# Output products of batches 0 to 6 as seven half-size products, and another order of the last batch's blocks, stores and products

## The chip, the cores and the metric

The kernel runs on one core of one Trainium2 chip. The metric is the device time of one launch in microseconds (us); lower is better. Engines: TensorE (PE, matrix products; its weight loads are listed as PEld), VectorE (DVE), ScalarE (ACT), GpSimd (POOL) and SyncE (SP, which here only issues transfers). Matrix products write to PSUM banks of 128 x 512 f32 numbers.

## The reference

Attention with shared queries, keys and values over 8 batches of 1024 tokens with 512 features and 8 heads, where a 0/1 mask says which tokens count; the result is added to the input. All is f32.

```python
xt = jnp.transpose(x, (0, 2, 1))                     # x: (8, 512, 1024)
q = xt @ Wq.T
qh = q.reshape(B, T, NH, dk).transpose(0, 2, 1, 3)   # NH = 8, dk = 64
scores = scale * jnp.einsum('bhqd,bhkd->bhqk', qh, qh)
logits = (scores * cmask + (1.0 - cmask) * NEG) * rmask
attn = jax.nn.softmax(logits, axis=-1)
ctx = jnp.einsum('bhqk,bhkd->bhqd', attn, qh)
out = ctx.transpose(0, 2, 1, 3).reshape(B, T, D) @ Wo.T
return x + jnp.transpose(out, (0, 2, 1))
```

A masked-out row gets the same mean value for all its keys, so the kernel works on the kept tokens of a batch (about half) and one token that stands for all others.

## The kernel before, in words

**Tokens.** Each batch has room for 544 tokens (SHORT): four blocks of 128 and a strip of 32 (block LAST), with 544/2 = 272 queries in each half. If a batch keeps more, a second program with 576 (LONG) runs instead; it is built from the same functions.

**Pairs.** Two heads (128 features) of one batch are a pair (b, pr): 32 pairs, pr from 0 to 3. One loop runs over them, and its order of instructions is written by hand; each engine works through its own queue in that order. A pair has five slots k = 0 to 4. In each slot PE makes the scores of one block of keys (L684, strip first: L706) and ACT their exponentials (L692). Between them `slots_of` lists other work by slot, of neighbouring pairs and batches: the projection of the pair after next (`project`, L598), its transposed values (L626), lengths and a bias from them (L645 to L667), the weighted values of the pair before (`begin_attend`, `go_on_attend`, `end_attend`, L730 and L748), the gathered tokens of the next batch (`collect`).

**Sums and contexts.** `invert` inverts a pair's sums of exponentials on DVE, sends the row through DRAM and reads it back on all partitions (row and rb, SP's queue). Two pairs later `contexts` (L859 to L868) multiplies the weighted values by it; the result cT holds 128 features x 544 tokens. For the pair before the last, `spread` does this with PE and ACT instead (L810, L817).

**Outputs.** `output(b, i)` multiplies block i of the four cT tiles with woT (the transposed Wo, 512 features; L883), ACT copies the PSUM bank to a tile oc (L892), and POOL's queue stores it to DRAM as od (L894). For a block of 128 tokens that is four matmuls with 512 columns each, for the strip 16 small ones with 128 columns, four side by side. Outputs of batch b - 1 run in slot 3 of pairs (b, 1): blocks 0, 1 and LAST; (b, 2): block 2; (b, 3): block 3. In the last batch, b = 7, they run in (7, 1) and (7, 2). PSUM banks come in two rings of two, tags t and a; weighted values use a, nearly all else t.

**Back to the input.** `load_rows` reads rows of x (transposed) into g, `fetch` (L977, POOL) gathers od by token and adds it to g in the transfer, `finish_blocks` (L947, DVE) transposes g back, and SP stores a batch (L954, list `rests`). Tables say which of the eight blocks goes where, by (pr, k): FETCH and FINISH for batch b - 2, and FETCH_LAST, FINISH_LAST, ROWS_LAST for batch 6 in the last batch. Ahead of each fetch `keep_step` (L974) makes POOL wait for that slot's exponentials.

**The end.** Batch 7 has no later pairs. In pair (7, 3) `begin_output` multiplies blocks with the first three cT tiles (L903) and ACT keeps the partial sums; after `attend_last`, `end_output` adds the last product (L919, DVE L927) and SP stores od (L933). Then eight gathers (L963), PE transposes (L992), additions to x (L993) and stores (L994).

## Time and profile before

| | |
|---|---|
| time, median of 3 runs | 656.38 us (655.18 to 656.91) |
| profiled execution, its own time | 656.09 us |
| its span in the profile | 654.4 us |
| busy: PE, DVE, ACT, POOL | 614.3, 359.8, 378.3, 211.1 us |
| DMA | 116.62 MB, mean 178 GB/s |

The profile is of one execution. The span is from the first to the last instruction recorded; 1.7 us of the execution's time lie outside it. Busy times are the union of an engine's instructions. In the timeline a row is a start, a duration, the engine, the line of the kernel, the operation with the tiles written and read, the count of instructions merged into the row, and in brackets how long the engine had been idle and what ended that. In the groups by line the columns are busy time, mean ns of one, and idle time before them with its causes.

### The profile page before, as it was taken

The numbers are of one execution on the slowest core, as the hardware profiler recorded it, in microseconds if no ns is written. First come the engines' busy times: TensorE is split into PE (matmuls) and PEld (weight loads), VectorE is DVE, ScalarE is ACT, GpSimd is POOL, SyncE is SP. The second block draws the span as 40 slices with busy tenths as digits, with TensorE's granted clock in tenths as the row PEclk, the third lists the DMA queues.
The fourth block names the chain that finished last, engine by engine and source line by source line (L and its number), as shares of the span: only waits on it lengthen the run. The fifth ranks groups of instructions, "written<-read, shape, count | busy, mean of one in ns | idle before, by whom it ended". The sixth has DMA issues, their size and how long they took to land. (4 is left out here: it accounts for less than half of the span.)

```text
span 654.4 us, 15913 instructions
## 1 busy us (share of the span) xinstructions
PE 614.3 (94%) x6078; PEld 380.5 (58%) x6078; DVE 359.8 (55%) x1034; ACT 378.3 (58%) x1004; POOL 211.1 (32%) x313
## 2 busy tenths in 40 slices
PE   4789799999999999999999999999999999998964
PEld 3756466656665666566665666566665666554323
DVE  6449556335465566746465558566575425444543
ACT  4266558754766577754776577664775556554400
POOL 5620400140067004830176004720275006305422
PEclk7799899999999999999999999999999999999985
DMA  7666612454588757977598756975795635566677
GB/s 237 187 199 166 233 57 67 141 168 133 147 178 214 244 172 186 180 246 230 172 182 257 228 173 155 199 244 187 196 179 164 198 102 94 111 162 188 112 220 219
DMA packets 94543, 116.62 MB, mean 178 GB/s; under 512 B 11911, under 2 KB 61639, under 8 KB 94462
## 3 DMA queue, kind: packets, MB, share of 16 engines
q1 hardware_dynamic: 74030, 75.20, 38.6%
q0 software_dynamic: 16208, 38.25, 25.2%
q10 hardware_dynamic: 4224, 2.10, 1.1%
q8 instruction: 49, 0.80, 0.5%
q14 instruction: 32, 0.26, 0.1%
HBM read 72.81 MB, written 42.70 MB: 177 GB/s over the span
## 5 line engine op out<-in xcount | busy, mean ns | idle before, releaser
L692 ACT ACTIVATE e<-s,bias 128x544 f32<-128x544 f32 x256 | 180.5, 710 | 75.6 <-PE s L684 58.9
L684 PE MATMUL s<-qT 64*64 64x272 f32 x2048 | 154.8, 398 | 6.5 <-ACT e L692 4.9
L748 PE MATMUL av<-e,v 64*64 64x272 f32 x1920 | 132.4, 392 | 0.0
L598 PE MATMUL pq<-xc,wqT 128*128 128x272 f32 x512 | 131.4, 401 | 0.0
L598 PEld LDWEIGHTS pq<-xc,wqT 128*128 128x128 f32 x512 | 93.3, 190 | 36.8 <-issue 21.0
L684 PEld LDWEIGHTS s<-qT 64*64 64x64 f32 x2048 | 77.2, 133 | 55.8 <-ACT e L692 13.4
L883 PE MATMUL po<-woT,cT 128*128 128x512 f32 (+1 forms) x448 | 108.9, 439 | 0.0
L894 POOL DMA_DIRECT2D od<-oc x56 | 30.2, 544 | 238.5 <-ACT oc L892 237.7
L977 POOL DMA_INDIRECT g<-od,block_origin x56 | 90.1, 1610 | 30.9 <-DVE ends L721 8.1
L748 PEld LDWEIGHTS av<-e,v 64*64 64x64 f32 x1920 | 76.6, 134 | 38.1 <-issue 2.1
L664 DVE TENSOR_REDUCE m<-pq 128x1 f32<-128x128 f32 x28 | 8.2, 292 | 132.0 <-ACT qT L610 107.5
L883 PEld LDWEIGHTS po<-woT,cT 128*128 128x128 f32 (+1 forms) x448 | 46.5, 149 | 54.6 <-issue 53.2
L608 ACT COPY qT<-pq 128x272 f32<-128x272 f32 x64 | 24.6, 385 | 69.7 <-PE pq L655 29.0
L947 DVE STREAM_TRANSPOSE xr<-g 128x512 f32<-128x512 f32 x56 | 57.9, 1099 | 7.6 <-DMA g<-od,block_origin 7.5
L645 DVE TENSOR_REDUCE len<-sq 128x10 f32<-128x640 f32 x32 | 25.8, 805 | 60.4 <-ACT sq L643 60.3
L974 POOL COPY step<-e 1x1 f32<-1x1 f32 x75 | 23.7, 316 | 90.7 <-ACT e L692 90.5
L692 ACT ACTIVATION_READ_ACCUMULATOR e<-s,bias 128x1 f32 x256 | 50.5, 197 | 0.0
L544 POOL DMA_INDIRECT xin<-xd,source x40 | 38.7, 968 | 16.6 <-issue 5.6
L892 ACT COPY oc<-po 128x512 f32<-128x512 f32 (+1 forms) x35 | 18.0, 515 | 44.0 <-PE po L883 43.5
L474 DVE STREAM_TRANSPOSE xt<-x 128x1024 f32<-128x1024 f32 x28 | 34.7, 1241 | 1.5 <-DMA xd<-xt 0.9
L532 DVE TENSOR_SCALAR_CACHE_REDUCE junk<-rank,key 128x1024 f32<-128x1024 f32 (+4 forms) x35 | 34.9, 998 | 0.0
L721 DVE CUSTOM_DVE_ANT_0 junk<-el,part 128x272 f32<-128x272 f32 x64 | 27.3, 427 | 6.6 <-ACT el L709 4.4
(175 smaller groups left out, 674.0 us busy)
## 6 DMA issues: line engine op xcount, KB each, us to landing
xd<-xt SPq DMA_DIRECT2D x120, 128.0 KB
x<-in_x_dram SPq DMA_DIRECT2D x56, 256.0 KB
g<-xd SPq DMA_DIRECT2D x56, 256.0 KB
out_dram<-xr SPq DMA_DIRECT2D x28, 512.0 KB
rb<-row SPq DMA_DIRECT2D x60, 160.0 KB
od<-oc POOLq DMA_DIRECT2D x28, 256.0 KB
rank<-ranks SPq DMA_DIRECT2D x6, 512.0 KB
x<-in_x_dram POOLq DMA_DIRECT2D x8, 256.0 KB
```

The source lines that it names most:

```text
L474: nc.vector.transpose(xt.rearrange("p k (d f) -> p k d f", d=ND), xs[b][r][:, :, at : at + n].rearrange("p d (k t) -> p k d t", t=Q),)
L532: nc.vector.tensor_scalar(junk[:, :n], rank[:, i * P :], key[:, col], 0.0, ALU.is_le, ALU.add, accum_out=found[:, col])
L544: nc.gpsimd.indirect_dma_start(out=xin[:n, :], out_offset=None, in_=xds[b], in_offset=bass.IndirectOffsetOnAxis(ap=searches[b][2][:n, i : ...
L598: nc.tensor.matmul(pq[:, :KH], wqT[:, d, pr * P : (pr + 1) * P], xcs[b][:, d, cols], start=(d == 0), stop=(d == ND - 1),)
L684: nc.tensor.matmul(ss[h][r * DK : (r + 1) * DK, hf, :KH], qT[heads[h], c * P + r * DK : c * P + (r + 1) * DK], qT[heads[h], queries[hf]], ...
L692: nc.scalar.activation(e[:, :, h, :], ss[h][:, :, :KH], AF.Exp, bias=bias, scale=SCALE, accum_out=sums[pair[1] % 2][:, h, c : c + 1],)
L721: nc.vector.tensor_tensor_reduce(junk[:, :KH], e[:, 0, h, :], parts[b], 1.0, 0.0, ALU.mult, ALU.add, ends[pr % 2][:, h : h + 1])
L748: nc.tensor.matmul(avs[pair][hf][head, :KH], v[keys, c, head], e[keys, hf, h, :], start=(c == 0 and not crossed), stop=(c == LAST - 1 and ...
L883: nc.tensor.matmul(po[k * n : (k + 1) * n, :w], cTs[b, pr][:, i * P : i * P + n], woT[:, pr, k * w : (k + 1) * w], start=(pr == 0), stop=( ...
L894: nc.gpsimd.dma_start(ods[b][places[i], k * w : (k + 1) * w], oc[k * n : (k + 1) * n, :w])
L947: nc.vector.transpose(xr.rearrange("p (d a) (t i) -> p a d t i", a=A, i=NT)[..., i], gs[b, i].rearrange("p (a d f) -> p a d f", a=A, f=Q),)
L977: nc.gpsimd.indirect_dma_start(out=gs[b, i], out_offset=None, in_=ods[b], in_offset=bass.IndirectOffsetOnAxis(ap=block_origin[:, b, i : i ...
```

## The change

The four whole blocks of a batch are a product of 512 tokens x 512 features by 512 x 512 weights. It is split into halves in all three directions, and seven products of half the size, with sums of inputs and outputs around them, take the place of eight (Winograd's form of Strassen's method). It is done for batches 0 to 6 in the SHORT program; the strip of 32 tokens keeps `output`, and batch 7 keeps its four blocks.

- `combine_weights`, once, in pair (1, 0): four differences of quarters of woT on POOL.
- `combine_tokens`: sums s1 to s4 of quarters of cT on DVE, two instructions each, in the tiles of tag xt; in (b, 1), slots 1, 1, 2 and 4.
- `product(b, i)`: eight passes in four matmuls with 256 columns, into one PSUM bank. ACT copies product 1; DVE adds each of the others (product 5 twice); four stores of 256 tokens x 256 features on POOL's queue. Products 1, 6, 7, 5 run in (b, 1), 2 and 3 in (b, 2), 4 in (b, 3). Product 1 is issued ahead of `add_features` (list `leads`). In (b, 1) the second half of the projection uses tag a.
- In the last batch all seven products of batch 6 run in (7, 1), and the strip too; the tables FETCH_SOON, FINISH_SOON, FETCH_LAST, FINISH_LAST and ROWS_LAST put transfers and transposes earlier; `spread` and `contexts` of pair (7, 2) go to slot 0 of (7, 3); the partial products go to slots 1, 2, 3, 4, 4 (before 1, 1, 2, 3, 4), and the strip's are made four side by side (`add_product`), with two of its four stores on ACT's queue.
- In all batches, blocks 4 and 5 of FINISH go from slot 2 to slot 3 of (b, 1).

```diff
         for k in range(parts):
             nc.gpsimd.dma_start(ods[b][places[i], k * w : (k + 1) * w], oc[k * n : (k + 1) * n, :w])
 
+    HALF = D // 2
+    both = {}
+    if n == SHORT:
+        for i in range(1, 5):
+            both["t", i] = keep.tile([P, 2, HALF], F32, name=f"t_{i}")
+
+    def combine_weights():
+
+        left = [woT[:, 0:2, 0:HALF], woT[:, 2:4, 0:HALF]]
+        right = [woT[:, 0:2, HALF:D], woT[:, 2:4, HALF:D]]
+        t1, t2, t3, t4 = (both["t", i] for i in range(1, 5))
+        nc.gpsimd.tensor_tensor(t1, right[0], left[0], ALU.subtract)
+        nc.gpsimd.tensor_tensor(t2, right[1], t1, ALU.subtract)
+        nc.gpsimd.tensor_tensor(t3, right[1], right[0], ALU.subtract)
+        nc.gpsimd.tensor_tensor(t4, t2, left[1], ALU.subtract)
+
+    def combine_tokens(b, i):
+
+        if i in (1, 3):
+            t = sb.tile([P, T // NQ // Q, P], F32, tag="xt", name=f"st_{b}_{i}", bufs=2)
+            t = t.rearrange("p k c -> p (k c)").rearrange("p (s j n) -> p s j n", s=2, j=2)
+            both["s", i], both["s", i + 1] = t[:, 0], t[:, 1]
+        for j in range(2):
+            early, late_ = cTs[b, j], cTs[b, 2 + j]
+            to = both["s", i][:, j, :]
+            upper, lower = slice(0, 2 * P), slice(2 * P, 4 * P)
+            if i == 1:
+                nc.vector.tensor_tensor(to, early[:, lower], late_[:, lower], ALU.add)
+            elif i == 2:
+                nc.vector.tensor_tensor(to, both["s", 1][:, j, :], early[:, upper], ALU.subtract)
+            elif i == 3:
+                nc.vector.tensor_tensor(to, early[:, upper], early[:, lower], ALU.subtract)
+            else:
+                nc.vector.tensor_tensor(to, late_[:, upper], both["s", 2][:, j, :], ALU.subtract)
+
+    def product(b, i):
+
+        def tokens(j, m):
+            cols = slice(m * P, (m + 1) * P)
+            if i in (3, 5, 6, 7):
+                return both["s", {3: 4, 5: 1, 6: 2, 7: 3}[i]][:, j, cols]
+            first = 2 * P if i == 4 else 0
+            cols = slice(first + m * P, first + (m + 1) * P)
+            return cTs[b, j if i == 1 else 2 + j][:, cols]
+
+        def features(j):
+            if i == 1:
+                return woT[:, j, 0:HALF]
+            if i == 2:
+                return woT[:, 2 + j, 0:HALF]
+            if i == 3:
+                return woT[:, 2 + j, HALF:D]
+            return both["t", {4: 4, 5: 1, 6: 2, 7: 3}[i]][:, j, :]
+
+        po = bank(f"po_{b}_{i}")
+        for m in range(2):
+            for j in range(2):
+                nc.tensor.matmul(
+                    po[:, m * HALF : (m + 1) * HALF],
+                    tokens(j, m),
+                    features(j),
+                    start=(j == 0),
+                    stop=(j == 1),
+                )
+
+        def new(name):
+            t = both[name] = sb.tile([P, D], F32, tag="oc", name=f"{name}_{b}", bufs=NC)
+            return t
+
+        def store(t, row, col):
+            rows = slice(END + row * 2 * P, END + (row + 1) * 2 * P)
+            nc.gpsimd.dma_start(
+                ods[b][rows, col * HALF : (col + 1) * HALF].rearrange("(m p) c -> p m c", p=P),
+                t.rearrange("p (m c) -> p m c", m=2),
+            )
+
+        add = nc.vector.tensor_tensor
+        if i == 1:
+            ods[b] = dr.tile([NK, D], F32, tag="od", name=f"od_{b}")
+            nc.scalar.copy(new("c11"), po)
+        elif i == 6:
+            add(new("c12"), po, both["c11"], ALU.add)
+        elif i == 7:
+            add(new("c21"), po, both["c12"], ALU.add)
+        elif i == 5:
+            add(new("c22"), po, both["c21"], ALU.add)
+            add(both["c12"], po, both["c12"], ALU.add)
+            store(both["c22"], 1, 1)
+        elif i == 2:
+            add(both["c11"], po, both["c11"], ALU.add)
+            store(both["c11"], 0, 0)
+        elif i == 3:
+            add(both["c12"], po, both["c12"], ALU.add)
+            store(both["c12"], 0, 1)
+        else:
+            add(both["c21"], both["c21"], po, ALU.subtract)
+            store(both["c21"], 1, 0)
+
     partials = {}
 
+    def add_product(b, i, pr, po, start, stop):
+
+        n = sizes[i]
+        parts = P // n
+        w = D // parts
+        tokens = cTs[b, pr][:, i * P : i * P + n]
+        if parts == 1:
+            nc.tensor.matmul(po, tokens, woT[:, pr, :], start=start, stop=stop)
+            return
+        in_order = woT[:, pr, :].rearrange("p (a d f) -> p d a f", a=A, d=ND)
+        for k in range(parts):
+            nc.tensor.matmul(
+                po[k * n : (k + 1) * n, :w],
+                tokens,
+                in_order[:, k * ND // parts : (k + 1) * ND // parts, :, :],
+                start=start,
+                stop=stop,
+            )
+
     def begin_output(b, i):
 
-        n = sizes[i]
         po = bank(f"pa_{b}_{i}")
         for pr in range(ND - 1):
-            nc.tensor.matmul(
-                po[:n, :],
-                cTs[b, pr][:, i * P : i * P + n],
-                woT[:, pr, :],
-                start=(pr == 0),
-                stop=(pr == ND - 2),
-            )
+            add_product(b, i, pr, po, pr == 0, pr == ND - 2)
+        w = D // (P // sizes[i])
         pa = sb.tile([P, D], F32, tag="xin", name=f"pa_{b}_{i}", bufs=NC)
-        nc.scalar.copy(pa[:n, :], po[:n, :])
+        nc.scalar.copy(pa[:, :w], po[:, :w])
         partials[i] = pa
 
     def end_output(b, i):
         n = sizes[i]
+        parts = P // n
+        w = D // parts
         if i == 0:
             ods[b] = dr.tile([NK, D], F32, tag="od", name=f"od_{b}")
         po = bank(f"po_{b}_{i}")
-        nc.tensor.matmul(
-            po[:n, :],
-            cTs[b, ND - 1][:, i * P : i * P + n],
-            woT[:, ND - 1, :],
-            start=True,
-            stop=True,
-        )
+        add_product(b, i, ND - 1, po, True, True)
         oc = sb.tile([P, D], F32, tag="oc", name=f"oc_{b}_{i}", bufs=NC)
-        nc.vector.tensor_tensor(
-            oc[:n, :].rearrange("p (d a f) -> p a d f", d=ND, a=A),
-            po[:n, :].rearrange("p (a d f) -> p a d f", d=ND, a=A),
-            partials[i][:n, :].rearrange("p (a d f) -> p a d f", d=ND, a=A),
-            ALU.add,
-        )
-        nc.sync.dma_start(ods[b][places[i], :], oc[:n, :])
+        if parts == 1:
+            nc.vector.tensor_tensor(
+                oc.rearrange("p (d a f) -> p a d f", d=ND, a=A),
+                po.rearrange("p (a d f) -> p a d f", d=ND, a=A),
+                partials[i].rearrange("p (a d f) -> p a d f", d=ND, a=A),
+                ALU.add,
+            )
+        else:
+            nc.vector.tensor_tensor(oc[:, :w], po[:, :w], partials[i][:, :w], ALU.add)
+        for k in range(parts):
+            queue = nc.scalar if k % 2 else nc.sync
+            queue.dma_start(ods[b][places[i], k * w : (k + 1) * w], oc[k * n : (k + 1) * n, :w])
 
     def in_blocks(t):
         return t.rearrange("(k f) (a n) -> a f k n", f=Q, a=A)
...
         if before:
             do(0, go_on_attend, before)
         due = []
-        if pr == 1 and b + 1 == B:
-            due = [0, 1]
-        elif pr > 0 and 0 < b < B - 1:
+        if pr == 1 and b + 1 == B and in_halves:
+            for k, i in ((1, 1), (1, 2), (2, 3), (3, 4)):
+                do(k, combine_tokens, b - 1, i)
+        elif pr == 1 and b + 1 == B:
+            due = [1, 2]
+            do(2, output, b - 1, 0)
+        elif pr > 0 and 0 < b < B - 1 and not in_halves:
             due = {1: (0, 1, LAST), 2: (2,), 3: (3,)}[pr]
+        halves = ()
+        if in_halves and 0 < b < B - 1:
+            halves = ((), (1, 6, 7, 5), (2, 3), (4,))[pr]
+            if pr == 1:
+                for k, i in ((1, 1), (1, 2), (2, 3), (4, 4)):
+                    do(k, combine_tokens, b - 1, i)
         if not new:
+            if halves and pr == 1:
+                leads[p] = [lambda: product(b - 1, 1)]
+                halves = halves[1:]
+            for i in halves:
+                do(3, product, b - 1, i)
+            if halves and pr == 1:
+                do(3, output, b - 1, LAST)
             for i in due:
                 do(3, output, b - 1, i)
+        if in_halves and p == ND:
+            do(0, combine_weights)
         if p == 0:
             do(0, project, behind, 1)
             do(1, values, behind)
...
             do(3, collect, b + 1, 3, None, "a")
             do(3, collect, b + 1, 4, by_vector)
             do(3, lengths_of, behind)
+            for i in halves:
+                do(3, product, b - 1, i)
             for i in due:
                 do(3, output, b - 1, i)
             do(3, project_with_top, 0)
...
             do(1, project_with_values)
             do(2, lengths_of, behind)
             do(2, end_attend, before)
-            do(3, project_with_top, 1)
+            if pr == 1 and b + 1 == B and in_halves:
+                for k, i in ((2, 1), (2, 6), (3, 7), (3, 5), (4, 2), (4, 3), (4, 4)):
+                    do(k, product, b - 1, i)
+            do(3, project_with_top, 1, "a" if halves and pr == 1 else "t")
         elif behind:
-            do(1, output, b - 1, LAST - 1)
             do(1, values, behind)
             do(2, lengths_of, behind)
             do(2, end_attend, before)
             do(3, bias_of, behind)
-            do(3, output, b - 1, LAST)
         if p == ND - 1:
             for d in range(ND):
                 do(3 + d // 2, turn_weights, woT, "wo", d, None, "at"[d // 2], True)
         if pr == 1 and b + 1 == B:
-            do(4, output, b - 1, 2)
+            if not in_halves:
+                do(4, output, b - 1, LAST - 1)
+            do(4, output, b - 1, LAST)
         if p + 1 == len(pairs):
             for i in range(NC):
-                do((1, 1, 2, 3, 4)[i], begin_output, b, i)
+                do((1, 2, 3, 4, 4)[i], begin_output, b, i)
         return todo
 
     def load_weights(w, nm, queue=None):
...
             (1, 0): (5,),
             (1, 1): (6, 7),
         }
-        FINISH = {(0, 4): (0, 1), (1, 1): (2, 3), (1, 2): (4, 5), (1, 4): (6, 7)}
-        FETCH_LAST = {(2, 4): (0, 1, 2), (3, 0): (3, 4, 5), (3, 1): (6, 7)}
-        FINISH_LAST = {(3, 1): (0, 1, 2), (3, 2): (3, 4, 5), (3, 3): (6, 7)}
+        FINISH = {(0, 4): (0, 1), (1, 1): (2, 3), (1, 3): (4, 5), (1, 4): (6, 7)}
+        FETCH_SOON = {(0, 0): (0,), (0, 1): (1,), (0, 2): (2,), (0, 3): (3, 4), (0, 4): (5, 6), (1, 0): (7,)}
+        FINISH_SOON = {(0, 2): (0,), (0, 3): (1,), (0, 4): (2,), (1, 0): (3, 4), (1, 1): (5, 6), (1, 2): (7,)}
+        FETCH_LAST = {(2, 0): (0,), (2, 1): (1, 2), (2, 2): (3, 4), (2, 3): (5, 6), (2, 4): (7,)}
+        FINISH_LAST = {(3, 1): (0, 1, 2, 3), (3, 2): (4, 5, 6, 7)}
         ROWS = {(2, 2): (0, 1), (2, 3): (2, 3), (3, 0): (4, 5), (3, 2): (6, 7)}
-        ROWS_LAST = {(2, 0): (0, 1, 2), (2, 1): (3, 4, 5), (2, 2): (6, 7)}
+        ROWS_LAST = {(1, 0): (0, 1, 2), (1, 1): (3, 4), (1, 2): (5, 6), (1, 3): (7,)}
         for p, pair in enumerate(pairs):
             b, pr = pair
             before = pairs[p - 1] if p else None
...
                         invert(before)
                     else:
                         inv = inverses(before)
-                if p + 1 == len(pairs):
-                    if k == 1:
-                        spread(before, inv)
-                        contexts(before)
+                if p + 1 == len(pairs) and k == 0:
+                    spread(before, inv)
+                    contexts(before)
                 if b > 1:
-                    for i in FETCH.get((pr, k), ()):
+                    for i in (FETCH if b + 1 < B else FETCH_SOON).get((pr, k), ()):
                         keep_step(pair, c)
                         fetch(b - 2, i)
                 if b + 1 == B:
...
                 for i in (GATHER if b else GATHER_LATER).get((pr, k), ()) if b + 1 < B else ():
                     keep_step(pair, c)
                     gather(b + 1, i)
+                if k == 3:
+                    for task in leads.pop(p, ()):
+                        task()
                 if k == 3 and p > 1 and pr in (1, 3):
                     to = b + 2 if pr == 3 else b + 1
...
                 if p == 1 and k == 4:
                     turn_places()
                 if b > 1:
-                    for i in FINISH.get((pr, k), ()):
+                    for i in (FINISH if b + 1 < B else FINISH_SOON).get((pr, k), ()):
                         finish_blocks(b - 2, i)
                 if b + 1 == B:
                     for i in FINISH_LAST.get((pr, k), ()):
...
                 issue_stores()
                 while rests:
                     rests.popleft()()
-                    if b + 1 < B:
+                    if b + 1 < B or pr == 1 and len(rests) == 2:
                         break
             if p == 0:
                 shared["all"] = False
```

More of the change, by code (lines that the diff above doesn't have):

```diff
@@ L304, in attention_of_all_tokens, with attention_of_kept_tokens @@
             outs.popleft()()
-def attention_of_kept_tokens(ctx, tc, x, mask, wq, wo, out, ident, wqT, woT, verdict, flag):
+def attention_of_kept_tokens(ctx, tc, n, x, mask, wq, wo, out, ident, wqT, woT, verdict, flag):
     nc = tc.nc
@@ L321, in attention_of_kept_tokens @@
     NQ = 4
+    in_halves = n == SHORT
     NC = -(-LONG // P)
@@ L1465, in kept_tokens @@
             early, late = attention_of_kept_tokens(
-                pools, tc, x, mask, wq, wo, out, ident, wqT, woT, verdict, flag
+                pools, tc, n, x, mask, wq, wo, out, ident, wqT, woT, verdict, flag
             )
```

1 line of the change is left out of this document (added).

## The prediction

> **What bounds the kernel now.** I read the page's busy times first, then busy time by stretches of 20 us, then the timeline of one middle pair, one engine after the other, and last the timeline of the final two pairs.
>
> ```profile
> span 654.4 us, 15913 instructions
> PE 614.3 (94%) x6078; PEld 380.5 (58%) x6078; DVE 359.8 (55%) x1034; ACT 378.3 (58%) x1004; POOL 211.1 (32%) x313
> 100.00:120.00 20.00, 19.45 (x237) 13.42 (x239) 13.15 (x39) 16.29 (x45) 0.00 (x0) 1.00 0.36 97
> 300.00:320.00 20.00, 19.96 (x189) 12.64 (x187) 10.39 (x32) 13.20 (x37) 0.85 (x2) 1.00 0.66 208
> 600.00:620.00 20.00, 18.02 (x86) 6.63 (x85) 11.58 (x18) 7.87 (x19) 11.58 (x14) 1.00 0.69 106
> ```
>
> The columns after the stretch are the busy times of PE, weight loads, DVE, ACT and POOL, then the granted clock and the DMA share. In the middle PE is busy 19.96 of 20 us at full clock while DVE has half its time free: every PE pass taken away there is time gained, as long as no new wait stands in PE's queue. From about 600 us on PE has gaps (18.02 of 20), and there waits count.
>
> **The seven products.** In the trace each f32 matmul of the code is two passes (the eight rows of L598 below are its four). These rows, PE in pair (4,3), two weight loads of 512-column passes, and PE and DVE in pair (4,1), give the passes and the place of the outputs:
>
> ```profile
> 318.04 2.00 PE L598 MATMUL pq<-xc,wqT 128*128 128x272 f32 x8
> 319.87 0.27 PE L655 MATMUL pq<-ident,top 128*128 128x128 f32 x1
> ...
> 205.18 0.19 PEld L883 LDWEIGHTS po<-woT,cT 128*128 128x128 f32 x1 [0.24 <-issue]
> 205.61 0.19 PEld L883 LDWEIGHTS po<-woT,cT 128*128 128x128 f32 x1 [0.24 <-issue]
> ...
> 335.61 0.69 PE L706 MATMUL s<-qT 64*64 64x272 f32 x8
> 340.46 0.60 PE L626 MATMUL v<-ident,qT 128*128 128x128 f32 x4
> 340.89 0.27 PE L626 MATMUL pq<-ident,qT 128*128 128x128 f32 x1
> 344.92 8.14 PE L883 MATMUL po<-woT,cT 128*128 128x512 f32 x48
> 353.00 2.10 PE L598 MATMUL pq<-xc,wqT 128*128 128x272 f32 x8
> ...
> 339.62 0.22 DVE L859 TENSOR_TENSOR rb<-rb 128x64 f32<-128x64 f32 x1 [2.68 <-issue]
> 344.13 0.08 DVE L721 DVE_READ_ACCUMULATOR2_ANT ends<- 128x1 f32 x1
> 344.13 2.05 DVE L947 STREAM_TRANSPOSE xr<-g 128x512 f32<-128x512 f32 x2
> 355.80 0.29 DVE L664 TENSOR_REDUCE m<-pq 128x1 f32<-128x128 f32 x1 [6.87 <-ACT qT L610]
> ```
>
> A 512-column pass takes 0.43 us (205.61 less 205.18), a 272-column pass 0.229 ((319.87 - 318.04)/8), a 128-column pass 0.108 ((340.89 - 340.46)/4). That is a straight line, so a 256-column pass takes 0.2156 us (0.229 less 16 columns at 0.201/240). A batch's four whole blocks are 32 long passes, 13.76 us; seven products of eight short passes are 12.07 us. Saved: 1.69 us a batch, 11.8 us for seven. The bounds are narrow: a short pass can hardly cost more than the 272-column one, which leaves 13.76 - 56 x 0.229 = 0.94 us a batch. The strip of 32 tokens stays as it is.
>
> The Trainium skill, page "TensorE: Matmul & The Clock Gate", section "Back-to-back issue gap", speaks against the change: in a stream of weight loads and matmuls it gives 81 ns for 128 columns and 131 ns for 512, so that half the columns would cost about three quarters of the time. By that rule 56 short passes would cost an estimated 18 us instead of 13.76, a loss of 4.2 us a batch. The trace goes against it: 0.108, 0.229 and 0.43 us grow as the columns do.
>
> **What the products add elsewhere.** The groups by line give the prices:
>
> ```profile
> L867 DVE TENSOR_TENSOR cT<-cT,rb 128x544 f32<-128x544 f32 x31 | 22.5, 725 | 1.2
> L859 DVE TENSOR_TENSOR rb<-rb 128x64 f32<-128x64 f32 x32 | 7.0, 219 | 16.0 <-DMA rb<-row 9.3 <-ACT rb L817 4.0 <-issue 2.7
> L927 DVE TENSOR_TENSOR oc<-po,pa 128x512 f32<-128x512 f32 x4 | 2.8, 691 | 1.1 <-PE po L919 1.1
> L892 ACT COPY oc<-po 128x512 f32<-128x512 f32 x28 | 16.2, 577 | 40.9 <-PE po L883 40.9
> L401 POOL TENSOR_SCALAR part<-count,kept 64x272 f32<-64x272 f32 x16 | 15.5, 970 | 5.3 <-DMA xin<-xd,source 4.7
> L894 POOL DMA_DIRECT2D od<-oc x56 | 30.2, 544 | 238.5 <-ACT oc L892 237.7
> ```
>
> - DVE: eight sums of tokens of 256 columns, 0.42 us each (between 0.219 and 0.725), and seven additions out of PSUM at 0.691: 8.2 us a batch, 57 us in all. 359.8 becomes 417, two thirds of the span. Not a bound as a share; what counts is the order in pair (b,1), below.
> - ACT: four copies of 0.577 become one, 1.7 us less a batch.
> - POOL: four stores before, four after, with rows of 1 KB for 2 KB. The combinations of the weights, once, in pair (1,0): four instructions, each 1.8 us (0.970 scaled from 272 to 512 columns) to twice that for two inputs, 7 to 15 us. The stretch 100 to 120 has POOL idle, and the first user comes at about 130. No cost.
>
> Pair (b,1) decides whether the saving arrives. PE starts the outputs 9.3 us into it (344.92 - 335.61); product 6 would be wanted at 346.65 and product 7 at 348.37. DVE is held until 339.62 by the row of inverses that comes through DRAM, and ends its sums of the probabilities at 344.21. Then follow the first four sums of tokens, up to 1.7 us (product 6 ready at 345.9), two transposes, 2.05, and two more sums, 0.85: product 7 ready at 348.8 at the worst, 0.4 us late; with the overlap that two transposes show (2.05 for two of 1.1) it is 347.8, in time. The later additions come out of DVE's 6.87 us of idle time before 355.80, and each frees its PSUM bank before the product after the next. The two transposes moved past them then run into the next pair, which takes them from idle time in front of its copies of tokens. ACT's qT copy in (b,3) now comes right behind four sums of features, with less PE work to cover them, and may be a little late. I take 0.2 us of waits a batch (0 to 0.5, and up to 1.3 if the row lands later than now): 1.2 us on six batches. Pair (b,3) keeps the gain: one product of 1.72 us for a block of 3.44. Six batches: 10.1 - 1.2 = 8.9 us.
>
> **The last two batches.** PE, DVE and POOL at the end:
>
> ```profile
> 579.24 3.70 PE L883 MATMUL po<-woT,cT 128*128 128x512 f32 x8
> 588.34 0.32 PE L655 MATMUL top<-ident,top 128*128 128x128 f32 x1 [0.54 <-DVE top L652]
> 588.59 1.08 PE L883 MATMUL po<-woT,cT 128*32 128x128 f32 x32
> 597.49 1.13 PE L684 MATMUL s<-qT 64*64 64x272 f32 x12 [0.81 <-ACT el L709]
> 602.74 3.70 PE L903 MATMUL pa<-woT,cT 128*128 128x512 f32 x8 [0.95 <-DVE cT L867]
> 615.14 2.76 PE L903 MATMUL pa<-woT,cT 128*32 128x512 f32 x6
> 620.28 1.31 PE L810 MATMUL rb<-ident,ris 128*64 128x128 f32 x20 [1.31 <-DVE ris L831]
> ...
> 618.19 1.10 DVE L947 STREAM_TRANSPOSE xr<-g 128x512 f32<-128x512 f32 x1 [0.16 <-DMA g<-od,block_origin]
> 598.27 1.70 POOL L977 DMA_INDIRECT g<-od,block_origin  x1 [5.82 <-DVE ends L721]
> 611.84 1.56 POOL L977 DMA_INDIRECT g<-od,block_origin  x1 [0.26 <-issue]
> 632.96 1.00 POOL L963 DMA_INDIRECT g<-od,origin  x1 [19.56 <-DMA od<-oc]
> ```
>
> Batch 6 saves its 1.69 us too, but all its products now lie in (7,1), and (7,2) loses the block at 579.24 and the strip at 588.59. Those covered PE while ACT made the exponentials and the lengths; without them PE waits for ACT, about 1 us more than the 0.54 of now. I keep 0.7 us (-1 to 1.7).
>
> Pair (7,3): spread of the inverses goes ahead of the first block's scores, so it fills the 0.81 us wait, and the scores and the first four partial passes cover DVE's work on cT: 0.95 goes to about 0.3. Together 1.5 us. The strip's partial product, 2.76 us, becomes 24 narrow passes that run four abreast, as the 32 at 588.59 that take 1.0: 0.75, saved 2.0. The wait of 1.31 stands because DVE is still transposing at 618.19, behind fetches that POOL begins at 598.27 and ends at 611.84. The fetches move one pair earlier, where POOL issues one in 1.94 us ((611.84 - 598.27)/7). From about 3.5 us into (7,2), when the last store should have landed, the eighth goes out 13.6 us later and lands 6.3 us after that (618.19 - 611.84), some 8 us into (7,3) if (7,2) lasts 16; the eight transposes are over about 610 on the clock of these rows, and the inverses wait for the last exponentials only: 1.3 saved. The strip's last product, two 512-column passes, becomes eight narrow ones: 0.6. Sum 5.4 us, all in front of the last gathers at 632.96, whose 21 us after that stay. The output stores of batch 6 move ahead as well, which can only empty the queue that the last od stores use. Bounds: 2.5 (narrow products only) to 6.5.
>
> **The sum.** 8.9 + 0.7 + 5.4 = 15.0 us off the profiled execution's 656.09 us (span 654.4 and 1.7 around it; the median of three is 656.38): 641.1.
>
> **Rivals.**
> - The waits in (b,1) eat half: the row of inverses lands about 1.3 us later against PE, since a batch is 1.7 us shorter while its DMA work is not. Against it: DMA is at 0.66, not full. About 1 us a batch lost: 647.
> - The tail stays: the fetches of batch 6 land too late and the inverses are held as now, and the end has other waits. 3 to 5 us lost: 645.5.
> - Slower: the row lands so late that product 6 and all behind it wait. It landed 4.0 us into (4,1) (339.62 - 335.61). PE begins to wait from about 4.5 to 5 us; 2.5 us of waiting in each of six batches, a landing at 7 us or later, uses up the whole 15. One us beyond that is 662. For it: 16.0 us of DVE idle time before L859. Against it: nothing that sets this row is moved.
> - The short passes keep a fixed cost: from 0.246 us a pass on (13.76/56) the products lose. At 0.32, three quarters of a long pass, 56 cost 17.9 us, 4.1 more a batch, 29 in seven, less 5 of the tail: 680. That the 272-column pass takes 0.229 all but excludes it. It is what the Trainium skill's rule above would come to.
> - The change doesn't act because the longer size runs: excluded, the rows show halves of 272, which is 544/2.
>
> **Chances.** Forecast 0.57; half eaten 0.19; tail stays 0.12; a draw within 0.3% (about 2 us, what a measurement of this kernel can tell) 0.03; slower by the row 0.07; by the passes 0.02. The first three are faster: 0.88. The forecast's own bounds are 638 (all of 11.8 and 6.5) to 645; to hold 8 in 10 the range takes in the first two rivals: 637.5 to 650.
>
> **What would show it.** Right: products of eight 256-column passes at 0.216 us; pairs (b,3) 1.7 us shorter and (b,1) no longer; no wait at the inverses near the end, gathers about 15 us earlier. Wrong: PE rows of products with idle time released by DVE, a later L859 in (b,1), DVE still transposing when the last exponentials end.

## The result

| | before | changed | ratio, 95% interval |
|---|---|---|---|
| first comparison | 655.78 us (654.66 to 656.91) | 645.85 us (644.12 to 647.41) | 0.986 (0.983 to 0.989) |
| again, in another group of runs (e5) | 650.43 us | 635.34 us | 0.9765 (0.9739 to 0.9792) |

The change makes the kernel faster: by 9.9 us in the first comparison, by 15.1 us when the same file ran again beside before (e5). The forecast was 641.1 us, 15.0 us less than the profiled execution of before. The two intervals don't overlap, so the difference between the two comparisons has a cause, and most of the experiments went into it. Unless something else is said, "after" is the profile of the first comparison (647.41 us, span 645.7).

### The profile page after: what moved, and what is told of

Read it like the earlier page. It is cut to its first block, busy times and chain, and to the rows that moved or that the text cites. A ratio compares the mean times of both kernels' runs of the same rounds, so it can differ in the third digit from the quotient of the medians.

```text
span 645.7 us, 16377 instructions
## 1 busy us (share of the span) xinstructions
PE 607.6 (94%) x6270; PEld 416.4 (64%) x6270; DVE 410.1 (64%) x1139; ACT 366.4 (57%) x983; POOL 223.5 (35%) x317
## 5 line engine op out<-in xcount | busy, mean ns | idle before, releaser
L749 PE MATMUL av<-e,v 64*64 64x272 f32 x1920 | 134.2, 394 | 0.0
L749 PEld LDWEIGHTS av<-e,v 64*64 64x64 f32 x1920 | 79.7, 134 | 35.7 <-issue 0.8
L968 POOL DMA_DIRECT2D od<-c x28 | 21.1, 755 | 221.9 <-DVE c L986 82.9
L1087 POOL COPY step<-e 1x1 f32<-1x1 f32 x77 | 27.3, 355 | 52.7 <-ACT e L693 52.2
L545 POOL DMA_INDIRECT xin<-xd,source x40 | 39.2, 979 | 16.7 <-DMA woT<-in_L_cond_Wq_dram 5.5
L954 PE MATMUL po<-t,st 128*128 128x256 f32 x168 | 40.0, 386 | 4.1 <-DVE c L978 2.9
L954 PEld LDWEIGHTS po<-t,st 128*128 128x128 f32 x168 | 30.9, 190 | 12.0 <-DVE c L978 4.5
L494 ACT ACTIVATE junka<-x 128x512 f32<-128x512 f32 x48 | 30.2, 630 | 1.1
```

The lines of the kernel that those rows point to most:

```text
L494: nc.scalar.activation(junk, xs[b][r][:, d, :], AF.Copy, accum_out=xbars[b][:, d, r : r + 1])
L545: nc.gpsimd.indirect_dma_start(out=xin[:n, :], out_offset=None, in_=xds[b], in_offset=bass.IndirectOffsetOnAxis(ap=searches[b][2][:n, i : ...
L749: nc.tensor.matmul(avs[pair][hf][head, :KH], v[keys, c, head], e[keys, hf, h, :], start=(c == 0 and not crossed), stop=(c == LAST - 1 and ...
L954: nc.tensor.matmul(po[:, m * HALF : (m + 1) * HALF], tokens(j, m), features(j), start=(j == 0), stop=(j == 1),)
```

## The profile after

The page's busy times of after, and busy time by the three stretches that the prediction showed of before:

```profile
span 645.7 us, 16377 instructions
PE 607.6 (94%) x6270; PEld 416.4 (64%) x6270; DVE 410.1 (64%) x1139; ACT 366.4 (57%) x983; POOL 223.5 (35%) x317
100.00:120.00 20.00, 19.45 (x219) 13.80 (x222) 13.62 (x36) 16.38 (x45) 5.03 (x4) 1.00 0.25 67
300.00:320.00 20.00, 19.96 (x205) 13.98 (x207) 11.77 (x34) 12.75 (x36) 1.94 (x3) 1.00 0.77 236
600.00:620.00 20.00, 20.00 (x161) 9.33 (x161) 10.59 (x22) 7.86 (x19) 0.77 (x1) 1.00 0.65 136
```

DVE has 50 us more work (359.8 before; forecast 417), ACT 12 less. The four combinations of the weights are POOL's 5.03 us in the first stretch, 1.28 us each, less than the 7 to 15 forecast. The stretch 600 to 620 has lost PE's gaps: 20.00 busy of 20 us, where before had 18.02.

To see where the 8.7 us between the two profiles lie, I took the length of each pair from the start of its strip's scores to the start of the next pair's. In us, after less before:

| pairs | after less before | forecast |
|---|---|---|
| (b,3), b = 1 to 6 | -1.71 each, -10.2 | -1.7 each |
| (b,1), b = 1 to 6 | +0.21, +1.59, +0.81, +2.20, +1.06, +0.83: +6.7 | +0.2 each |
| (b,2), b = 1 to 6 | +0.02, then +0.17 to +0.20: +0.9 | 0 |
| (7,1) and (7,2) | +3.15 and -3.80: -0.65 | -0.7 |
| (7,3) to the end | 58.82 to 51.92: -6.9 | -5.4 |
| (0,2), and all ahead of the first pair | +0.72 and +0.77 | 0 |

One term is far off: the waits in (b,1). Pair (4,1) of after starts at 334.91. Its timeline, first PE, then ACT, then DVE (start, duration, engine, line; in brackets how long the engine had been idle and what ended that):

```profile
344.23 1.99 PE L954 MATMUL po<-woT,cT 128*128 128x256 f32 x8
346.06 1.89 PE L954 MATMUL po<-t,st 128*128 128x256 f32 x8
348.51 1.99 PE L954 MATMUL po<-t,st 128*128 128x256 f32 x8 [0.56 <-issue]
351.56 1.99 PE L954 MATMUL po<-t,st 128*128 128x256 f32 x8 [1.06 <-DVE c L978]
...
345.69 0.20 ACT L693 ACTIVATION_READ_ACCUMULATOR e<-s,bias 128x1 f32 x1
347.87 0.58 ACT L976 COPY c<-po 128x512 f32<-128x512 f32 x1 [1.98 <-remote]
...
346.60 0.16 DVE L653 TENSOR_REDUCE top<-len 128x1 f32<-128x10 f32 x1
350.81 0.69 DVE L978 TENSOR_TENSOR c<-po,c 128x512 f32<-128x512 f32 x1 [4.05 <-PE po L954]
351.60 0.69 DVE L980 TENSOR_TENSOR c<-po,c 128x512 f32<-128x512 f32 x1
```

Products 1, 6, 7 and 5 of batch 3, eight passes each. Product 1 ends at 346.22 (344.23 and 1.99), and ACT is free since 345.89, but its copy begins at 347.87, 1.65 us late, and no releaser that the profile knows stands at the end of the wait ("remote"). Product 6 ends at 347.95, DVE is free since 346.76, and its addition begins at 350.81, 2.86 us late. (The addition also reads the copy, which ends at 348.46; 2.36 us are left from there.) Products 7 and 5 use the banks of products 1 and 6 again, so PE waits until the copy and the addition are over (348.46 and 351.51). The waits for DMAs that stand in front of the copy in ACT's queue had passed by 345.02. So neither the row of inverses nor DVE's order explains this pair, although they were what the prediction watched.

## The experiments

Three theories stood at the start. S: while GpSimd issues the gathers of the next batch's tokens, which fall into the same stretch, an engine's signal that an instruction has ended reaches the others late. D: DVE's transposes and sums stand in the way. R: the row of inverses lands later. The experiments e1 to e4 ran on one chip, e5 to e8 on a second, e9 to e12 on a third, each group in one session and beside before on its chip. Which chip the first comparison ran on is not on record.

**e1: the end alone.**

```diff
-    in_halves = n == SHORT
+    in_halves = False
```

> Batches 1 to 6 make their outputs in whole blocks as in the kernel before; all that the change does around the last batch (tables, order of blocks, narrow strip, spread first) stays. If the end alone gave what the trace of the changed kernel shows from the start of (7,3) (58.82 to 51.92 us), this is about 7 us under before; by my prediction's terms 5.4 us. Pairs (b,1) and (b,3) are as long as before (21.6 and 16.9 us). If the products gave nothing, it is as fast as the changed kernel (about 10 us under before).

645.32 us against 651.78, ratio 0.9913 (0.9882 to 0.9943). Pairs (b,1) and (b,3) are as long as before to 0.01 us. So the end and the order around it give 6.5 us by the medians and 5.7 by the ratio.

**e2: the gathers later.**

```diff
-        GATHER = {(1, 2): (0, 1), (1, 3): (2, 3, 4)}
+        GATHER = {(1, 4): (0, 1, 2), (2, 0): (3,), (2, 1): (4,)}
```

> The changed kernel with the five gathers of the next batch's tokens moved from slots 2 and 3 of (b,1) to slot 4 of (b,1) and slots 0 and 1 of (b,2). Theory S (while GpSimd issues gathers, the signal that a product has ended reaches ACT and DVE 1 to 2.8 us late, so the two PSUM banks come free late): the copy of product 1 starts within 0.1 us of its end (now 0.9 to 1.7 late), the waits of PE in front of products fall from 8.0 us to 2 or less, pairs (b,1) are 1 us shorter on the mean, and the total is about 15 us under before. Theory D (DVE's transposes and sums of tokens stand ahead of the additions) and theory R (the row of inverses lands later): nothing changes, about 10 us under before.

643.36 us, ratio 0.989 (0.9856 to 0.9925). The copy of product 1 now begins 0.04 us behind its end in every batch, and the six pairs (b,1) are 0.9 us over before in all. (Of the waits of 8.0 us in the expectation, the profile of after shows 4.1 us as idle time of PE in front of products; the pairs grew by 6.7.) But the five pairs (b,2) of batches 2 to 6 grow by 1.1 to 1.6 us each, 6.9 in all. In (4,2), PE's timeline says why: the transposes of the gathered tokens wait for them to land.

```profile
358.45 1.41 PE L558 MATMUL xc<-ident,xin 128*128 128x128 f32 x8
360.28 1.63 PE L558 MATMUL xc<-ident,xin 128*128 128x128 f32 x12 [0.41 <-DMA xin<-xd,source]
361.83 2.00 PE L954 MATMUL po<-woT,cT 128*128 128x256 f32 x8
```

They take 3.4 us in place of 2.4. The gathers stood where they did for a reason. By itself e2 seemed to speak for S.

**e3: four banks for the products.**

```diff
-        po = bank(f"po_{b}_{i}")
+        po = bank(f"po_{b}_{i}", "a" if i in (5, 7) else "t")
...
-            do(3, project_with_top, 1, "a" if halves and pr == 1 else "t")
+            do(3, project_with_top, 1, "t")
```

> The changed kernel with products 7 and 5 in the two banks of tag a, and the projection's second half back in tag t, so that four banks serve the four products of (b,1). Theory S: the copy of product 1 and the addition of product 6 start as late as now (0.9 us and more behind the ends of their products), but PE does not wait for them: waits in front of products 2 us or less, total 13 to 15 us under before. Theory D: product 7 still waits for its sum of tokens, total 10 to 11 us under before. Theory R: unchanged, about 10.

635.51 us, ratio 0.9773 (0.9735 to 0.9811). The time is better than S had it, but for another reason: with the gathers in their old place the copy of product 1 was not late at all, 0.04 us in all six batches. The six pairs (b,1) are 1.9 us over before: in three of them product 7 starts late, as in theory D. S as I had put it, as a property of this program, fell here.

**e4: plain transfers for the gathers.**

```diff
-        nc.gpsimd.indirect_dma_start(out=xin[:n, :], ...)
+        if 1 < b:
+            nc.gpsimd.dma_start(xin[:n, :], xds[b][i * P : i * P + n, :])
```

> The changed kernel with the gathers of the tokens of batches 2 to 7 replaced by plain transfers of the same tiles and sizes at the same places of GpSimd's queue (the first rows of each batch instead of the kept ones, so the choice of tokens is left out). Theory S, in the form that only indirect transfers hold back the signals: copy of product 1 within 0.1 us of its end, waits in front of products 2 us or less, total about 15 us under before. If any transfer that GpSimd issues does it, or theory D or R holds: lateness and waits as now, about 10 us under before.

635.4 us, ratio 0.9752 (0.9726 to 0.9779): with e3 about equal, and the six pairs (b,1) 1.1 us over before. Since the signals were prompt with and without indirect gathers on this chip, it tells nothing on them.

I then counted signals. The trace has the times at which PE, ACT and DVE raise their semaphores. Of those that are due within 0.3 us of the issue of an indirect transfer, 35% have no such record within 0.1 us in the profiles of before and after (589 and 650 signals); of those beside GpSimd's plain transfers none, and elsewhere 0.4 and 0.7%. In e1 to e4 it is 0.8% or less everywhere. Some of the 35% are records that are missing only, since a waiter went on at once; but waits that end in "remote" occur in before and after and in none of e1 to e4. In all of before, and in all of after:

```profile
ACT e L692 <- remote: 5.5, 1, 5.5
```

```profile
ACT e L693 <- remote: 5.2, 1, 5.2
ACT c L976 <- remote: 2.0, 1, 2.0
DVE c L978 <- remote: 0.4, 1, 0.4
```

The 5.5 and 5.2 us are in pair (0,2), which takes 23.7 and 24.4 us there and 18.2 to 19.1 in e1 to e4. So the lateness seemed to belong to the chip or the moment and not to the change, and before paid for it in one place only. Before's own times fit that: 655.78 us in the first comparison, 651.78 and 650.43 beside e1 to e4 and e5 to e8.

**e5: the changed kernel again.** No edit.

> The changed kernel as it is, again, because in the four runs so far no signal of an engine came late beside GpSimd's gathers, while in the first profile of the changed kernel a third of them did. If the late signals belong to the chip or the moment and not to the program: copy of product 1 within 0.1 us of its end, waits in front of products about 2 us in all (the part that DVE's order makes), pairs (b,1) 0.3 us over before on the mean, total 14 to 16 us under before. If they belong to this program: as in the first profile, waits of 8 us, total about 10 under before.

635.34 us against 650.43, 15.1 less, ratio 0.9765: no late signal (0.2%), no "remote" wait, pair (0,2) at 18.4 us. In pair (4,1), which starts at 326.09, PE and ACT:

```profile
335.41 2.00 PE L954 MATMUL po<-woT,cT 128*128 128x256 f32 x8
337.24 5.34 PE L954 MATMUL po<-t,st 128*128 128x256 f32 x24
...
337.44 0.58 ACT L976 COPY c<-po 128x512 f32<-128x512 f32 x1 [0.37 <-PE po L954]
```

The same program at the same places: the copy follows the end (337.41) by 0.03 us, and three products run without a gap. What is left in the six pairs (b,1) is 2.4 us, nearly all in (2,1), (3,1) and (5,1). Pair (5,1) starts at 396.88; DVE, then PE:

```profile
402.57 0.22 DVE L860 TENSOR_TENSOR rb<-rb 128x64 f32<-128x64 f32 x1 [4.37 <-DMA rb<-row]
408.27 2.03 DVE L1060 STREAM_TRANSPOSE xr<-g 128x512 f32<-128x512 f32 x2
410.16 0.72 DVE L928 TENSOR_TENSOR st<-cT 128x256 f32<-128x256 f32 x2
...
408.07 1.99 PE L954 MATMUL po<-t,st 128*128 128x256 f32 x8
410.70 3.57 PE L954 MATMUL po<-t,st 128*128 128x256 f32 x15 [0.64 <-DVE st L928]
```

Here the row of inverses lands 5.7 us into the pair, and product 7 waits for the sum that stands behind two transposes. That is the chain that the prediction described (D and R together): 0.4 us a batch for 0.2 forecast, within its range of 0 to 0.5. The prediction's mark for the row holds too, a wait from 4.5 to 5 us on: rows at 4.97, 4.80 and 5.69 us lengthen their pairs by 0.5, 0.6 and 1.2 us, rows at 4.04 us and earlier by 0.04.

**e6: the third sum ahead of the transposes.**

```diff
-                for k, i in ((1, 1), (1, 2), (2, 3), (4, 4)):
+                for k, i in ((1, 1), (1, 2), (1, 3), (4, 4)):
```

> The changed kernel with the third sum of tokens of (b,1) in slot 1 in place of 2, so ahead of DVE's two transposes. Theory D (product 7 waits for its sum because DVE transposes first): product 7 no longer waits for DVE, but product 5 still waits for the addition of product 6 out of the bank; 0.5 to 2 us under the changed kernel on the same chip. If late signals hold the banks: no change.

635.24 us, ratio 0.9761 (0.9733 to 0.9789). As D said, product 7 starts at 12.87 us in every pair. In three pairs product 5 now starts late instead (0.3 to 0.8 us), behind the addition of product 6. The six pairs are 2.1 us over before. Against e5 no difference that can be measured.

**e7: the four banks again.** The kernel of e3.

> The kernel of e3 once more, beside the changed kernel on one chip. If only late signals made the banks matter, it equals the changed kernel within 0.3% on a chip without them and is 4 to 6 us faster on one with them. If the banks matter by themselves: 1 to 3 us faster on any.

634.5 us, ratio 0.975 (0.9722 to 0.9779). The pairs (b,1) are 0.3 us over before in all (the same kernel had 1.9 in e3), but the time is that of e5 within its interval.

**e8: both edits.**

> Both edits, e3's four banks and e6's early sum. Theory D with late signals as an extra: pairs (b,1) as long as before (21.6 us) on any chip, no wait in front of a product over 0.1 us, 1.7 us saved in each of six pairs (b,3); total 17 us under before, the fastest of the four. If something else holds products 7 and 5: as e3.

636.16 us, ratio 0.9776 (0.9743 to 0.9809). All six pairs (b,1) at 21.61 to 21.67 us and no wait in front of a product, as D has it. But the row came at 4.5 us into the pair or earlier in all six, and in e7, without the early sum, rows at up to 4.6 us cost 0.1 us; that the early sum did it is not shown. Nor is e8 the fastest: the 2.2 us that it saves in (b,1) are less than what else varies between executions of one kernel here (633.0 to 638.3).

**e9 to e11: late on purpose.** To show on any chip what lateness costs, results leave their banks late: e9 does it in the changed kernel, e10 in that of e3, e11 in before.

```diff
-            nc.scalar.copy(new("c11"), po)
+            c11 = new("c11")
+            for _ in range(4 if b < B - 2 else 1):
+                nc.scalar.copy(c11, po)
```

(the same for the addition of product 6, and in before for the copies of blocks 0 and 1)

> The changed kernel with the results of products 1 and 6 of batches 0 to 5 taken out of their banks late on purpose: ACT's copy of product 1 and DVE's addition of product 6 are done four times over, so a bank comes free 1.75 and 2.1 us later, about the lateness of the signals in the first profile. Theory B (with two banks and products of 1.72 us the change leaves no room for a late signal): product 7 starts at 13.5 us into (b,1) for 12.87, product 5 at about 16.2 for 14.60, each pair (b,1) 1.6 us longer, 9 to 10 us in six, total 5 to 6 us under before. Against it (the late signals of the first profile cost their time elsewhere): less than 3 us more than the changed kernel.

> The same delays in the kernel with four banks. Theory B: products 7 and 5 start at 12.87 and 14.60, pairs (b,1) as without the delays, total 15 to 16 us under before. Against it: as e9.

> The kernel before with the same delay on ACT's copies of blocks 0 and 1 of batches 0 to 5 (four times over, 1.75 us each). Theory B: a block takes PE 3.44 us, so two banks leave room for it; pairs (b,1) stay at 21.6 us and the time at that of before, within 0.3%. Against it: 1 to 2 us more in each of six pairs.

This chip has late signals too: about a third (32 to 36%) beside indirect transfers, "remote" waits in all four profiles, (0,2) at 20.8 to 21.5 us. Against 654.16 us of before:

| kernel | us | ratio (interval) | six pairs (b,1) over before |
|---|---|---|---|
| e9, two banks, delayed | 659.19 | 1.0055 (1.002 to 1.009) | 23.1 us |
| e10, four banks, delayed | 643.6 | 0.9859 (0.981 to 0.9907) | 4.1 us |
| e11, before, delayed | 664.17 | 1.017 (1.0125 to 1.0215) | 9.5 us |
| e12, two banks, not delayed | 646.78 | 0.9892 (0.9851 to 0.9934) | 6.4 us |

Pair (3,1) of e9, which starts at 265.68, PE, ACT and DVE:

```profile
276.83 1.89 PE L954 MATMUL po<-t,st 128*128 128x256 f32 x8
280.47 1.99 PE L954 MATMUL po<-t,st 128*128 128x256 f32 x8 [1.75 <-issue]
283.46 1.97 PE L954 MATMUL po<-t,st 128*128 128x256 f32 x8 [1.00 <-DVE c L982]
...
277.98 2.44 ACT L978 COPY c<-po 128x512 f32<-128x512 f32 x4 [1.32 <-PE po L954]
...
280.44 2.87 DVE L982 TENSOR_TENSOR c<-po,c 128x512 f32<-128x512 f32 x4 [1.79 <-PE po L954]
```

The same picture as in the first profile, now with a known cause on top: products 7 and 5 start at 14.8 and 17.8 us for the 13.5 and 16.2 expected, because the late signals add to the delays. So e9 is 5 us slower than before, where 5 to 6 us under it was expected. In pair (4,1) of e10, which starts at 329.71, the first copy begins 1.22 us late and the first addition 1.25 us behind the last copy, so signals come late on top of the delays, and the products run without a wait. The projection behind the strip is what waits now:

```profile
340.85 5.34 PE L954 MATMUL po<-t,st 128*128 128x256 f32 x24
346.12 1.08 PE L884 MATMUL po<-woT,cT 128*32 128x128 f32 x32
348.94 2.07 PE L599 MATMUL pq<-xc,wqT 128*128 128x272 f32 x8 [1.73 <-DVE c L982]
...
342.24 2.44 ACT L978 COPY c<-po 128x512 f32<-128x512 f32 x4 [1.55 <-PE po L954]
345.93 2.87 DVE L982 TENSOR_TENSOR c<-po,c 128x512 f32<-128x512 f32 x4 [4.30 <-PE po L954]
```

So lateness at the banks costs PE time, as theory B says, and more than it says: the delays add 16.7 us to the six pairs (23.1 for e12's 6.4), where 9 to 10 were expected. Two more banks take most of it away: with late signals and delays together e10 loses less in (b,1) than e12 with late signals alone. Theory B failed for before: I expected no loss, and each pair (b,1) lost 1.58 us. In (4,1) of e11, PE:

```profile
350.83 4.61 PE L883 MATMUL po<-woT,cT 128*128 128x512 f32 x40
356.95 2.10 PE L598 MATMUL pq<-xc,wqT 128*128 128x272 f32 x8 [1.51 <-ACT oc L893]
```

Blocks and strip run on without a gap; the projection behind the strip waits. The last copy of block 0 ends 3.15 us behind its block, less than the 3.43 us that block 1 takes, and costs nothing. The copies of block 1 end 2.5 us behind it, more than the strip takes, and the projection, which needs that bank, waits. So the room of a bank here is the time of the product that follows in the other one.

That before pays nothing for the chip's own late signals in its pairs (b,1) (21.57 to 21.63 us) has another reason as well. In pair (4,1) of before, ACT and then POOL:

```profile
349.37 0.57 ACT L892 COPY oc<-po 128x512 f32<-128x512 f32 x1
352.09 0.58 ACT L892 COPY oc<-po 128x512 f32<-128x512 f32 x1 [2.16 <-PE po L883]
...
349.98 0.89 POOL L544 DMA_INDIRECT xin<-xd,source  x1 [0.16 <-issue]
```

Block 0 ends while gathers are issued, but its copy stands behind other work of ACT until 0.74 us after that. Block 1 ends at 352.06, 1.2 us after the last gather's issue, and its copy follows by 0.03 us. The change lets three products (1, 6 and 7) end while gathers are issued. How much of its loss comes from that and how much from the smaller room was not separated: e2, which moves the gathers, ran only on a chip without late signals.

**e12: the spread back in slot 1.**

```diff
-                if p + 1 == len(pairs) and k == 0:
+                if p + 1 == len(pairs) and k == 1:
                     spread(before, inv)
...
-                do((1, 2, 3, 4, 4)[i], begin_output, b, i)
+                do((1, 1, 2, 3, 4)[i], begin_output, b, i)
```

> The changed kernel with the spread of the inverses back in slot 1 of (7,3), behind the first block's scores, and the partial products back in slots 1, 1, 2, 3, 4. If this part is worth the 1.5 us of my sum, the two waits of before (0.81 and 0.95 us) come back and (7,3) is 1.5 to 1.8 us longer than in the changed kernel (52.1 us), all before its last weighing. If the partial products cover it either way: under 0.5 us.

Pair (7,3) to the end takes 55.20 us for 51.92 in after (52.01 and 52.79 in e9 and e10 on the same chip). PE at its start and at the inverses:

```profile
591.91 1.13 PE L685 MATMUL s<-qT 64*64 64x272 f32 x12 [0.86 <-ACT el L710]
597.05 3.70 PE L1004 MATMUL pa<-woT,cT 128*128 128x512 f32 x8 [0.85 <-DVE cT L868]
...
612.05 1.31 PE L811 MATMUL rb<-ident,ris 128*64 128x128 f32 x20 [0.66 <-DVE ris L832]
```

The two waits of before are back (0.81 and 0.95 there): the last weighing starts 1.85 us later in the pair than in after. The expectation "all before its last weighing" was too narrow: 0.9 us more go at the inverses and behind them, and 0.5 us behind the last products. The 0.5 are no more than what the profiles with the changed end differ by there (22.8 to 23.8 us from the last product to the end).

## Why the prediction was right, and where not

- *What bounds the kernel, and the passes: right.* All six pairs (b,3) are 1.71 us shorter, the saving of 1.69 us; short passes cost what the line through the other sizes gave (in e5 product 7 starts 1.72 us behind product 6).
- *DVE, ACT, POOL as shares: right.* No share became a bound; the combinations of the weights were cheaper than the lower end.
- *The waits in (b,1): mis-sized.* The sum had 1.2 us for six batches. After measured 6.7, and 0.9 in (b,2), so the six batches gave 2.6 us (10.2 less 7.6) for 8.9. The step that failed is the sentence "each frees its PSUM bank before the product after the next". It took for granted that ACT and DVE learn of a product's end at once. There they learned it up to 2.9 us late, beside gathers in which three of the products end, and a product of 1.72 us with two banks leaves less room than a block of 3.44 us. Without late signals the term measured 2.4 us, with the chain and the place that the prediction named. The 0.9 us in (b,2), put at nothing, are there with and without late signals: the transposes of the gathered tokens take 2.40 to 2.45 us in (2,2) to (6,2) of after and e5 for 2.26; why is not shown.
- *Batch 6: right.* -0.65 for -0.7 us.
- *The end: right in its parts, 1.5 us too small.* From the start of (7,3), the first of the last weighings comes 3.8 us earlier (forecast 3.5 for cover and strip; e12 puts 1.85 on the cover for 1.5). The wait at the inverses goes, 1.5 for 1.3; the strip's last product gives 0.6 as forecast. Not seen was 1.05 us between the last product and the first gathered block: these rows of after stand against 631.77 and 636.69 of before.

```profile
594.80 1.31 PE L811 MATMUL rb<-ident,ris 128*64 128x128 f32 x20
596.05 1.15 PE L685 MATMUL s<-qT 64*64 64x272 f32 x16
611.46 0.86 PE L1008 MATMUL pa<-woT,cT 128*32 128x128 f32 x24
613.22 1.26 PE L811 MATMUL rb<-ident,ris 128*64 128x128 f32 x20
624.04 0.27 PE L1546 MATMUL worst_t<-ident,worst 128*1 128x128 f32 x1 [1.26 <-DVE worst L1544]
627.91 1.09 PE L1105 MATMUL o<-ident,g 128*128 128x128 f32 x4 [3.60 <-DMA g<-od,origin]
```

  The stretch from the last product to the first gathered block takes 5.05 to 5.17 us in every profile with the changed end, 6.18 and 6.41 in before and e11. No run took that apart; the change also splits the strip's stores over two queues there.
- *The rivals.* "The waits in (b,1) eat half" (647) is what the first comparison shows, but not by its mechanism: of (2,1) to (6,1) the pair that grew most, (4,1), has its row earliest, 2.4 us into the pair (the others 4.1 to 5.1). By its own mechanism it is a part of the 2.4 us in e5. The row did not land 1.3 us later: over (2,1) to (6,1) it came at 3.3, 3.7 and 4.0 us on the mean with the order of before (before, e11, e1), at 4.0 and 4.4 in after and e5. The tail did not stay, the wait at the inverses is gone. The slower rival and the one of the passes did not occur.

So the sign, the passes and the end were read rightly from the trace of before. That the total without late signals is 15.1 us for the 15.0 forecast (e5) is in part luck: by the lengths of e5's pairs the six batches give 6.9 us for 8.9 and the end 6.7 for 5.4, and the two misses partly cancel. The time itself, 635.34 us, lies under the range of 637.5 to 650, because before is faster there too. What the trace of before did hold, unread, was the "remote" wait of 5.5 us in pair (0,2). It showed that a signal can come late.

Open: what makes the signals late, and whether that belongs to the chip or to the moment; no chip is known to have been measured in two sessions. Four banks without delays were not run on a chip with late signals, so how much of the 6.4 us they give back there is not measured.

## What to carry to other kernels

When work is cut into smaller pieces that pass through the same number of banks, the slack of each bank shrinks with the piece: work out how late a reader may be before the producer waits, and hold it against the longest unexplained wait in the trace, not against zero. A wait in the profile that no releaser explains is a warning, even where it costs nothing now. And before a difference between two runs is put down to the program, run the same file beside the old one on another chip and at another time.

## What the chip showed that was not expected

In the first comparison and on the chip of e9 to e12 about a third of the signals of PE, ACT and DVE that are due beside GpSimd's indirect transfers come late or have no record. It holds beside both kinds: 52 and 58% beside the gathers of tokens in before and after, 28 and 24% beside the fetches of od. In pairs (b,1) of after, copies of product 1 and additions of product 6 that waited on an idle engine started 0.7 to 2.9 us behind the end of the product, and in pair (0,2) ACT stood 5.2 us. On the two chips of e1 to e8 it is under 1%. Beside plain transfers on the same queue no signal is late: 0 of 137 and 0 of 156 in the profiles of before and after. The landings of DMAs split in the same way: 8382 to 8481 have a record in each profile with late signals, 9741 to 9833 in each of the others, of 656 or 659 transfers that each kernel issues with several landings each; whether the rest came late or only lack a record is not known. The Trainium skill, page "Perfetto Trace Analysis", section "Per-engine timelines", puts the way of a signal to the other engines behind an instruction's end, outside of what the profile shows, and gives no length for it. The rows here give one: 0.03 to 0.04 us from the end of product 1 to the start of its copy in e2 to e8.
